# Own-chunk attention scores packed into half-width columns, in a scheduled four-layer kernel

## The chip, the cores and the metric

The program runs on one NeuronCore of a Trainium2 chip. A core has five engines with instruction queues of their own: TensorE (PE in the profile, with its weight loads apart as PEld), VectorE (DVE), ScalarE (ACT), GpSimd (POOL) and SyncE (SP, which here only issues DMAs). Each engine takes its instructions in order; between engines there are semaphores. The metric is the device time of one execution, in microseconds (us); lower is better.

## The reference

The input is x of 4 sequences, 512 positions, 128 channels. Four layers follow each other, each added to its input after a layer norm:

1. a power attention with 16 heads of 8 channels and a decay by gates;
2. a mixture of 8 experts (128 to 352 to 128 channels, each token goes to 2 of them);
3. a gated linear recurrence (called hgrn in the kernel);
4. the mixture of experts again, with the same weights.

The change is in the first layer. What it computes, cut to what matters:

```python
qkvgr = jnp.einsum('btc,oc->bto', x, W)          # q, k, v and one gate per head
log_G = jnp.cumsum(log_sigmoid(gates), axis=1)   # per head, over positions
S = jnp.einsum('bhtd,bhsd->bhts', Q, K)
Z = 2 * jnp.log(jnp.abs(S) + 1e-7) + log_G[..., :, None] - log_G[..., None, :] + const
Z = jnp.where(tril(ones((T, T))), Z, -inf)       # a target t sees the sources s <= t
P = jnp.exp(Z - rowmax)
y = einsum('bhts,bhsd->bhtd', P, V) / P.sum(-1)
```

Since the exponential undoes the logarithm, P is (|S| + 1e-7) squared times exp(log_G[t] - log_G[s]), up to a factor of the row that the division takes out. The kernel computes it in this form.

## The kernel before

**The plan.** All work is written as operations (`op`, L61) with the engines that may run it, a cost on each, what it reads and writes, and a priority. `Plan.run` (L138) writes out the instructions in an order that it finds with clocks of its own: `choose` (L200) gives an operation to the engine that would end it first by these costs plus `BIAS` (L26; DVE carries 0.3 us), and takes among those that can start the one with the lowest priority value. `room`, `pick` and `take` keep the buffers: kinds k2, k4, dec and others are lists of SBUF tiles, b1 is one of eight PSUM banks, b2 a pair of banks. An operation that opens a buffer waits in the plan until one is free. When PE would be idle for long in the plan, `lull` writes filler matmuls (L195). So costs, biases, priorities and buffer counts only decide the order and the engines; what runs then is fixed.

**Gates (`gates`, L583).** For each of the 4 sequences: layer norm, transposes, q, k, v and gates, the cumulated logs in three bf16 terms. These go through DRAM (`gd`) into the tile `gs` (L655, eight loads on SP's queue), which holds them as rows of a matmul with 6 rows, so that the matmul yields log_G[t] - log_G[s]. v stands in a tile `v` with 9 columns a head, the ninth being 1, for the norm. For sources of earlier chunks `vo` holds v with its decays multiplied in (L663).

**Attention (`attend`, L677).** A sequence has 4 chunks of 128 positions. `attend(b, g)` treats 4 heads of a sequence, one in each group of 32 partitions (L683 masks k for that); there are 16 attends, each released by the end of the one two before (`done`, L681). Scores lie with sources on partitions and targets in columns, heads in two pairs. The steps of one attend:

- `decay(half)` (L687), twice: a bf16 matmul puts the causal mask of 4 x 128 columns into a PSUM pair (L692), eight matmuls of 6 rows add the decay differences of the own chunk (L696), ACT takes the exponent of 2 x 512 columns into a `dec` tile (L701). A half stands for two chunks and all four heads.
- `scores(rnd)` (L707), three rounds: matmuls (L717) of source chunk 0 against all 4 target chunks (512 columns a head); of chunk 1 against 1 to 3 and chunk 3 against 3 (512); of chunk 2 against 2 and 3 (256). For each pair of heads the magnitude is taken out of PSUM by ACT (L728) or DVE (L729), and ACT squares it in place (L733).
- `fade(rnd, pr)` (L738): own-chunk columns are multiplied by the decays, in pieces of 2 x 128 columns on DVE or POOL (L744 and L749; eight in one attend).
- `values(jobs)` (L757): matmuls with v of 18 columns (two heads side by side) sum the result, own chunks into one PSUM bank (L771), earlier chunks into another (L775); six groups in one attend. Every second attend transposes and normalizes (from L806 to L842).

Own chunks are computed as full 128 x 128 squares, of which the mask leaves the lower triangle.

**The rest.** `route` (L863) places tokens by expert and sends them by indirect DMA on POOL (L1002); `experts` (L1040) runs up to 20 blocks of 128 tokens in each of 4 passes (L1088 first matmuls, L1107 transposes, L1112 second matmuls, L1125 the indirect DMA that sends results back); `combine` and `hgrn` (L1160) follow. The first pass of experts begins while the last sequence is in attention.

## Time and profile before

| | |
|---|---|
| time, median of 6 runs | 494.14 us (492.18 to 498.25) |
| the profiled execution | 494.13 us, span 492.4 us |
| PE busy | 428.6 us, 87% of the span |
| ACT busy | 341.2 us, 69% |
| DVE busy | 295.7 us, 60% |
| POOL busy | 246.6 us, 50% |
| attention's last square (L733) starts | 220.8 us |

The span runs from the first to the last instruction; the time is a little longer than it. Busy shares are means over the whole span, in which attention (the first 222 us or so) and the expert layers have different limits. A group in the profile names the line, the engine, the operation, what is written and read (partitions x columns) and how often; behind it stand busy time and the mean of one instruction, then the idle time ahead of them and who ended it. "issue" is idle time in which the engine waited for nothing that the profile shows. Buffer numbers are left out: a tile of k2 or k4 is called k, a PSUM bank ps. Records of fp32 matmuls come in twos for one matmul of the code.

### The profile page before, as it was taken

Reading aid. Unit: us, or ns where it says so; the run is one execution under the profiler, and the core shown is the slowest. Engines: PE = TensorE matmul, PEld = TensorE weight load, DVE = VectorE, ACT = ScalarE, POOL = GpSimd, SP = SyncE. Lnnn points to the kernel's source line nnn. Section 1 sums busy time; section 2 is a strip of 40 time slices with the busy share of each in tenths; the row PEclk is TensorE's granted clock in tenths of the full one; section 3 lists DMA queues with packets and bytes.
Section 4 is the critical chain, followed back from the end, with each engine's and each line's share of the span. In section 5 each row is a group of like instructions: output and inputs, shape, how many; then the busy total and the mean of one; then the engine's idle time right before and its main releaser. Section 6 shows DMA issues by size and latency. Waiting matters only on the chain.

```text
span 492.4 us, 10857 instructions
## 1 busy us (share of the span) xinstructions
PE 428.6 (87%) x3776; PEld 294.0 (60%) x3803; DVE 295.7 (60%) x896; ACT 341.2 (69%) x610; POOL 246.6 (50%) x399
## 2 busy tenths in 40 slices
PE   8899888878879889889899999979899989699960
PEld 7554445534545446447788767658666757478750
DVE  7865676857777687856721577880187894051212
ACT  5778999989987999997755564854445675146530
POOL 6353252563336322833488543488743567835540
PEclk9979999999998999999999999998989999799995
DMA  3047200174004910100113410012430011361004
GB/s 102 5 111 181 70 1 1 44 209 61 2 12 121 207 21 3 49 2 13 38 57 107 123 34 5 13 54 73 112 113 7 16 34 49 102 173 49 28 19 133
DMA packets 47070, 31.48 MB, mean 64 GB/s; under 512 B 6144, under 2 KB 44958, under 8 KB 47008
## 3 DMA queue, kind: packets, MB, share of 16 engines
q1 hardware_dynamic: 39232, 20.69, 17.8%
q0 software_dynamic: 4608, 8.44, 5.2%
q10 hardware_dynamic: 3168, 1.57, 1.1%
q8 instruction: 33, 0.54, 0.5%
q14 instruction: 29, 0.24, 0.2%
HBM read 15.73 MB, written 16.00 MB: 64 GB/s over the span
## 4 chain that ended last, share of the span: by engine, by line
PE 21%; POOL 15%; DVE 13%; issue 13%; ACT 12%; DMA 3%; POOLq 0%; DVEq 0%; SPq 0%; ACTq 0%
POOL yg L1125 8%; PE ps L1088 7%; ACT k L733 5%; PE ps L1112 4%; POOL xg L1002 3%; PE ps L1107 3%; ACT k L728 3%; PE ps L1169 2%; DMA k<-yg 2%; PE ps L717 1%; ACT dec L701 1%; POOL dummy L853 1%; DVE k L729 1%; ACT k L359 1%; POOL st L1211 1%
## 5 line engine op out<-in xcount | busy, mean ns | idle before, releaser
L1125 POOL DMA_INDIRECT yg<-y,xb x80 | 80.6, 1007 | 66.2 <-ACT y L1118 56.5
L1088 PE MATMUL ps<-we,k 128*128 x320 | 110.2, 472 | 1.1 <-issue 0.5
L733 ACT ACTIVATE k<-k,aeps 128x1024 f32<-128x1024 f32 (+1 forms) x96 | 92.0, 1006 | 0.8 <-DVE k L729 0.2
L1103 DVE TENSOR_TENSOR k<-k,ps 128x352 f32<-128x352 f32 x80 | 40.3, 515 | 84.5 <-PE ps L1088 82.6
L1002 POOL DMA_INDIRECT xg<-xk,slt x64 | 65.7, 1026 | 42.2 <-DVE slt L996 11.6
L359 ACT COPY k<-ps 128x384 f32<-128x384 f32 (+1 forms) x122 | 60.4, 511 | 35.9 <-PE ps L1107 20.4
L1112 PEld LDWEIGHTS ps<-we,k 128*128 128x128 f32 (+1 forms) x480 | 63.5, 196 | 11.9 <-ACT k L359 2.2
L1088 PEld LDWEIGHTS ps<-we,k 128*128 128x128 f32 x320 | 56.4, 194 | 23.1 <-issue 3.3
L1112 PE MATMUL ps<-we,k 128*128 (+1 forms) x480 | 66.8, 282 | 0.9 <-ACT k L359 0.6
L717 PE MATMUL ps<-k,k 32*128 32x384 f32 (+3 forms) x512 | 59.6, 474 | 3.0 <-ACT dec L701 1.3
L728 ACT ACTIVATE k<-ps 128x1024 f32<-128x1024 f32 (+1 forms) x53 | 47.4, 913 | 9.9 <-PE ps L717 9.9
L1100 ACT ACTIVATE k<-ps 128x352 f32<-128x352 f32 x77 | 35.4, 462 | 20.6 <-PE ps L1088 18.6
L729 DVE TENSOR_SCALAR k<-ps 128x1024 int32<-128x1024 int32 (+1 forms) x43 | 42.0, 982 | 11.5 <-PE ps L717 10.7
L744 POOL TENSOR_TENSOR k<-k,dec 128x256 f32<-128x256 f32 x30 | 26.5, 896 | 43.6 <-ACT k L733 34.9
L775 PE MATMUL ps<-k,vo 128*18 128x128 f32 x768 | 40.7, 283 | 8.0 <-ACT k L733 6.5
L1118 ACT ACTIVATE y<-ps 128x128 f32<-128x128 f32 x78 | 21.4, 277 | 36.9 <-PE ps L1112 34.0
L1107 PE MATMUL ps<-ident,k 128*128 128x128 f32 (+1 forms) x240 | 38.6, 281 | 7.6 <-DVE k L1103 4.0
L717 PEld LDWEIGHTS ps<-k,k 32*128 32x128 f32 x512 | 28.8, 186 | 19.1 <-ACT dec L701 4.7
L1107 PEld LDWEIGHTS ps<-ident,k 128*128 128x128 f32 (+1 forms) x240 | 27.9, 140 | 15.7 <-DVE k L1103 6.1
L775 PEld LDWEIGHTS ps<-k,vo 128*18 128x18 f32 x768 | 21.3, 99 | 24.9 <-ACT k L733 18.0
L771 PE MATMUL ps<-k,v 128*18 128x128 f32 x512 | 29.9, 285 | 5.6 <-POOL k L749 3.2
L701 ACT ACTIVATE dec<-ps 128x1024 f32<-128x1024 f32 x32 | 32.2, 1018 | 3.5 <-PE ps L696 3.0
(193 smaller groups left out, 640.3 us busy)
## 6 DMA issues: line engine op xcount, KB each, us to landing
xb<-xg SPq DMA_DIRECT2D x20, 258.0 KB
xg<-zero SPq DMA_DIRECT2D x8, 451.5 KB
k<-yg SPq DMA_DIRECT2D x12, 256.0 KB
we<-in_L_ffn_w_dram SPq DMA_DIRECT2D x8, 352.0 KB
xg<-zero SPq DMA_DIRECT2D x4, 387.0 KB
yg<-y,xb POOLq DMA_INDIRECT x80, 2.2
x<-in_L_attn_a_x_dram SPq DMA_DIRECT2D x4, 256.0 KB
we<-in_L_ffn_w_dram SPq DMA_DIRECT2D x8, 128.0 KB
```

Of the source, the lines that this page charges most:

```text
L359: e.copy(dst, src)
L717: e.matmul(sps[hh // 2].t[:, hh % 2, c : c + tn * P], kT.t[r, s * P : (s + 1) * P], qT.t[r, t0 * P : (t0 + tn) * P], start=True, stop=True)
L728: e.activation(view(), sps[pr].t[:, :, 0:n], AF.Abs)
L729: if e is nc.scalar else e.tensor_scalar(view().bitcast(I32), sps[pr].t[:, :, 0:n].bitcast(I32), 0x7FFFFFFF, None, ALU.bitwise_and)
L733: op({"ACT": act(2 * n)}, lambda e, pa=pa: e.activation(pa.t, pa.t, AF.Square, bias=aeps.t), r=[pa, aeps], w=[(pa, "o"), (pa, "d")], pri=p ...
L775: e.matmul(oo.t[rows, (i - 1) * P : i * P], s, p, start=(ev == 0 and (i, j) == (1, 0)), stop=(ev == 1 and j == i - 1), skip_group_check=True)
L1002: d = e.indirect_dma_start(out=xgv.t, out_offset=bass.IndirectOffsetOnAxis(ap=slot.t[:, k * NB + n : k * NB + n + 1], axis=0), in_=xk[k].t ...
L1088: e.matmul(ph.t[:, w, 0:HID], xT.t[:, k * P : (k + 1) * P], wf[:, bass.ds(regs[j] + w * HID, HID)], start=True, stop=True)
L1103: op({"DVE": ve(HID, True) + 0.03}, lambda e, ph=ph, sl=sl, h=h: e.tensor_tensor(h.t[:, 0:HID], sl.t[:, 0:HID], ph.t[:, 1, 0:HID], ALU.mul ...
L1107: e.transpose(hp.t[0:fn, f0 : f0 + P], h.t[:, f0 : f0 + fn], ident.t) for f0, fn in FCH
L1112: e.matmul(hp.t[:, NF_ * P : NF_ * P + C], hT.t[0:fn, kk * P : (kk + 1) * P], wf[0:fn, bass.ds(regs[j] + 2 * HID + kk * C, C)], start=(kk ...
L1125: d = e.indirect_dma_start(out=ygv.t, out_offset=bass.IndirectOffsetOnAxis(ap=xb.t[:, k, C : C + 1].bitcast(I32), axis=0), in_=y.t, in_off ...
```

## The change

Of an own chunk's square, the first 64 targets can see only the first 64 sources. The change computes, for each chunk, the last 64 targets against all 128 sources, and the first 64 targets against the first 64 sources; the latter fill only 64 partitions, so that those of an even and an odd chunk lie in the same columns, one on partitions 0 to 63, one on 64 to 127. Four own chunks take 4 x 64 + 2 x 64 = 384 columns a head in place of 512. With it change:

- the rounds: two of 512 columns; the columns of (3, 2) stand beside the own chunks, (2, 1) beside chunk 0's; (3, 1) goes into the 128 columns that are now spare in each decay pair, with a small tile (kind k1) of its own, whose magnitude only ACT takes;
- the decays: a half now stands for two heads with all own chunks; mask, exponent and `dec` tiles have 384 columns a head; `gs` is loaded by head and not by chunk;
- the fades: one per pair of heads, 2 x 384 columns;
- a tile `vs`: v of the first 64 positions of each chunk, for odd chunks on partitions 64 to 127 (four copies per sequence, and its memsets at the start); own-chunk values are 32 matmuls of 64 columns in one group, `near`;
- the plan: DVE's bias of 0.3 goes; operations of attention carry a term `lean` on one engine: 0.6 on ACT for magnitudes, 0.3 on ACT where else ACT is a choice, 0.3 on DVE where DVE and POOL are; several buffers of one kind are now looked for together; costs of PE, ACT and DVE are changed; exponents, spare magnitudes and squares get other priorities; k2 tiles are 12 and not 16, dec tiles 4 and not 3 (smaller).

The diff, without some cost constants, and from `ROUND` on without the removed lines (they stand in the kernel before):

```diff
-BIAS = {"PE": 0.0, "DVE": 0.3, "ACT": 0.0, "POOL": 0.0, "SP": 0.0}
+BIAS = {"PE": 0.0, "DVE": 0.0, "ACT": 0.0, "POOL": 0.0, "SP": 0.0}
...
+        self.lean = {}
...
-                n2 = [v for v in need if v.kind == "b2"]
-                if ok and len(n2) > 1 and len(self.room(n2[0])) < len(n2):
+                alike = [[v for v in need if v.kind == c] for c in {v.kind for v in need}]
+                alike = [vs for vs in alike if len(vs) > 1]
+                if ok and any(len(self.room(vs[0])) < len(vs) for vs in alike):
                     ok = False
                 if not ok:
                     if keep and at <= now + 2.0:
                         kept |= groups
                     continue
-                if len(n2) > 1:
-                    at = max(at, sorted(a for a, _, _, _ in self.room(n2[0]))[len(n2) - 1])
+                for vs in alike:
+                    at = max(at, sorted(a for a, _, _, _ in self.room(vs[0]))[len(vs) - 1])
                 for v in need:
                     at = max(at, self.pick(v, at)[0])
-            e = min(o.engs, key=lambda e: max(clock[e], at) + o.engs[e] + BIAS[e])
+            e = min(o.engs, key=lambda e: max(clock[e], at) + o.engs[e] + BIAS[e] + o.lean.get(e, 0.0))
...
+    vst = many("vs", 2, [P, NB, NH // 2, 3, HV])
+    HP, W3 = P // 2, 3 * P
...
-            "k2": many("k2_", 16, [P, T]),
+            "k2": many("k2_", 12, [P, T]),
+            "k1": many("k1_", 5, [P, 2 * P]),
             "k4": many("k4_", 6, [P, 2 * T]),
-            "dec": many("dec", 3, [P, 2 * T]),
-            "v": vt, "vo": ot, "gs": gst, "pad": padt,
+            "dec": many("dec", 4, [P, 2 * W3]),
+            "v": vt, "vs": vst, "vo": ot, "gs": gst, "pad": padt,
...
     def ve(n, ps=False):
-        return 0.12 + n * (0.00098 if ps else 0.0009)
+        return 0.14 + n * (0.00104 if ps else 0.0009)
 
     def act(n):
-        return 0.215 + n * 0.00071
+        return 0.16 + n * 0.00084
 
...
-    op({"DVE": ve(T)}, lambda e: e.tensor_copy(
-        negm4.t, negm.t.unsqueeze(1).to_broadcast([P, 4, P])), r=[negm], w=[negm4], pri=INIT)
+    op({"DVE": 0.35}, lambda e: e.tensor_copy(
+        negd.t[:, 0 : 2 * P].rearrange("p (n c) -> p n c", c=HP),
+        negm.t[:, HP:P].unsqueeze(1).to_broadcast([P, 4, HP])), r=[negm], w=[(negd, 2)], pri=INIT)
+    for h in range(2):
+        op({"DVE": 0.22}, lambda e, rows=slice(h * HP, (h + 1) * HP): e.tensor_copy(
+            negd.t[rows, 2 * P : W3].rearrange("p (n c) -> p n c", c=HP),
+            negm.t[rows, rows].unsqueeze(1).to_broadcast([HP, 2, HP])), r=[negm], w=[(negd, h)], pri=INIT)
...
+        for k, t in enumerate(vst):
+            op({"POOL": 0.9}, lambda e, t=t: (
+                e.memset(t, 0.0), e.memset(t[0:HP, 0::2, :, 0::2, HS:HV], 1.0),
+                e.memset(t[HP:P, 1::2, :, 0::2, HS:HV], 1.0)),
+               w=[slots_v[14 + k]], pri=INIT + 20 * k, after=mark)
...
+        for n in range(NB):
+            at = slice(n % 2 * HP, n % 2 * HP + HP)
+            op({"DVE": 0.27} if n % 2 else either(P), lambda e, n=n, at=at: copy(
+                e, vs.t[at, n, :, 0::2, 0:HS],
+                p4()[0:HP, n, 0:P].rearrange("p (m e d) -> p m e d", e=2, d=HS)),
+               r=[pr] + slots_v[14:16], w=[(vs, n)], pri=pri)
...
-        gv = lambda t: t.rearrange("p (g j n) -> p g j n", g=NG, n=NB)
-        ge = lambda: pg.t[:, 0:n0].rearrange("p (n j g) -> p g j n", n=NB, g=NG)
+        gv = lambda t: t.rearrange("p (j g n) -> p j g n", g=NG, n=NB)
+        ge = lambda: pg.t[:, 0:n0].rearrange("p (n j g) -> p j g n", n=NB, g=NG)
...
-            rows = lambda n=n: gd.t.rearrange("(h n) r t -> n r h t", n=NB)[n]
+            rows = lambda n=n: gd.t.rearrange("(j h) r t -> j r h t", j=4)[n]
             for u in range(2):
                 r0 = 32 * n + 3 * u
                 mark = sp(lambda e, r0=r0, u=u, rows=rows: e.dma_start(
-                    out=gs.t[r0 : r0 + 3, u].rearrange("p g (j t) -> p (g j) t", t=P), in_=rows()),
+                    out=gs.t[r0 : r0 + 3, u].rearrange("p g (n t) -> p (g n) t", t=P), in_=rows()),
...
+
+
+    NEAR = [(n * P, P, n * P + HP, 0, n * HP) for n in range(NB)]
+    NEAR += [(n * P, HP, n * P, n % 2 * HP, 2 * P + n // 2 * HP) for n in range(NB)]
+    ROUND = (
+        [(s0, sn, t0, HP, p0, c) for s0, sn, t0, p0, c in NEAR] + [(2 * P, P, W3, P, 0, W3)],
+        [(0, P, P, W3, 0, 0), (P, P, 2 * P, P, 0, W3)],
+    )
+    AT = {(1, 0): (1, 0), (2, 0): (1, P), (3, 0): (1, 2 * P), (2, 1): (1, W3), (3, 2): (0, W3), (3, 1): (2, 0)}
...
+        tiles = {}
+
+        def square(rnd, pa, n):
+            op({"ACT": act(n) + 0.13}, lambda e: e.activation(pa.t, pa.t, AF.Square, bias=aeps.t),
+               r=[pa, aeps], w=[(pa, "o"), (pa, "d")], pri=pri - 0.55 + 0.2 * rnd)
+
         def decay(half):
+
             pd = new("b2")
 
             def go(e):
                 for k in range(2):
...
+                    e.matmul(pd.t[:, k, 0:W3], identb.t, negd.t, start=True, stop=False)
+                for s0, sn, t0, p0, c in NEAR:
                     for k in range(2):
...
+                        r = 32 * (2 * half + k)
+                        e.matmul(pd.t[p0 : p0 + sn, k, c : c + HP], gs.t[r : r + 6, 0, g, s0 : s0 + sn],
+                                 gs.t[r : r + 6, 1, g, t0 : t0 + HP], start=False, stop=(c == 2 * P + HP))
+                for k in range(2):
+                    r = slice(32 * (2 * half + k), 32 * (2 * half + k) + 32)
+                    e.matmul(pd.t[:, k, W3:T], kT.t[r, P : 2 * P], qT.t[r, W3:T], start=True, stop=True)
+
+            pa = new("k1")
+            tiles[2, half] = (pa, lambda: pa.t.rearrange("p (u c) -> p u c", u=2))
+            op({"PE": 1.2}, go,
+               r=[identb, negd, kT, qT] + [(gs, (2 * half + k, u)) for k in range(2) for u in range(2)],
+               w=[pd], pri=pri - 0.4, after=start, hold=[dec[half], pa])
+            exps.append(op({"ACT": act(2 * W3)}, lambda e: e.activation(
+                dec[half].t.rearrange("p (k c) -> p k c", k=2), pd.t[:, :, 0:W3], AF.Exp),
+               r=[pd], w=[dec[half]], pri=pri - 1.4, table=("ln", "exp")))
+            op({"ACT": act(2 * P)}, lambda e: e.activation(tiles[2, half][1](), pd.t[:, :, W3:T], AF.Abs),
+               r=[pd], w=[pa], pri=pri - 1.4)
+            square(2, pa, 2 * P)
 
         def scores(rnd, pri):
...
+            n = T
             sps = [new("b2") for _ in range(2)]
...
+            pas = [new("k4") for _ in range(2)]
 
             def go(e):
...
+                for s0, sn, t0, tn, p0, c in ROUND[rnd]:
                     for hh in range(4):
                         r = slice(32 * hh, 32 * hh + 32)
...
+                        e.matmul(sps[hh // 2].t[p0 : p0 + sn, hh % 2, c : c + tn],
+                                 kT.t[r, s0 : s0 + sn], qT.t[r, t0 : t0 + tn], start=True, stop=True)
+
+            op({"PE": 0.95}, go, r=[kT, qT], w=sps, pri=pri, after=start, hold=pas)
             for pr in range(2):
                 pa = pas[pr]
                 view = lambda pa=pa: pa.t.rearrange("p (u c) -> p u c", u=2)
                 tiles[rnd, pr] = (pa, view)
...
+                mags.append(op(either(2 * n), lambda e, pr=pr, view=view: (
                     e.activation(view(), sps[pr].t[:, :, 0:n], AF.Abs)
                     if e is nc.scalar else e.tensor_scalar(
                         view().bitcast(I32), sps[pr].t[:, :, 0:n].bitcast(I32), 0x7FFFFFFF, None,
                         ALU.bitwise_and)
...
+                ), r=[sps[pr]], w=[pa], pri=pri + 0.05))
+                square(rnd, pa, 2 * n)
             return n
 
...
+        def fade(pr, pri):
+            pa, view = tiles[0, pr]
+            op({"DVE": ve(2 * W3) + 0.1, "POOL": 2.4}, lambda e: e.tensor_tensor(
+                view()[:, :, 0:W3], view()[:, :, 0:W3], dec[pr].t.rearrange("p (u c) -> p u c", u=2), ALU.mult),
+               r=[dec[pr], (pa, "d")], w=[(pa, "d")], pri=pri)
 
         if ev == 0:
             accs[b, m] = (new("b1"), new("b1"))
         od, oo = accs[b, m]
 
+        def lanes(t, k, hh):
+            return t[:, k, 2 * hh + m].rearrange("p k w -> p (k w)")[:, HV * ev : HV * ev + 2 * HV]
+
+        def near(pri):
+
+            jobs = [(vs, n, 2 * P + n // 2 * HP, 2 * n) for n in range(NB)] + [(v, n, n * HP, 2 * n + 1) for n in range(NB)]
+
+            def go(e):
+                for x, n, c, to in jobs:
+                    for hh in range(4):
+                        e.matmul(od.t[32 * hh : 32 * hh + 2 * HV, to * HP : (to + 1) * HP],
+                                 lanes(x.t, n, hh), tiles[0, hh // 2][1]()[:, hh % 2, c : c + HP],
+                                 start=(ev == 0 and to == 0), stop=(ev == 1), skip_group_check=True)
+
+            return op({"PE": 1.0}, go, r=[(tiles[0, pr][0], "d") for pr in range(2)] + [v, vs], w=[od], pri=pri)
+
         def values(jobs, pri):
...
             def go(e):
                 for i, j in jobs:
                     rnd, c = AT[i, j]
                     for hh in range(4):
...
+                        e.matmul(oo.t[32 * hh : 32 * hh + 2 * HV, (i - 1) * P : i * P],
+                                 lanes(o.t, pairs.index((i, j)), hh),
+                                 tiles[rnd, hh // 2][1]()[:, hh % 2, c : c + P],
+                                 start=(ev == 0 and (i, j) == (1, 0)),
+                                 stop=(ev == 1 and j == i - 1), skip_group_check=True)
+
+            return op({"PE": 0.26 * len(jobs)}, go, r=[(tiles[AT[j][0], pr][0], "o") for j in jobs for pr in range(2)] + [o],
+                      w=[oo], pri=pri)
 
         decay(0)
...
+        scores(0, pri - 1.0)
         decay(1)
...
+        scores(1, pri - 0.8)
         for pr in range(2):
...
+            fade(pr, pri)
+        values([(1, 0), (2, 0), (3, 0), (2, 1)], pri)
+        near(pri + 0.1)
+        done[n_] = values([(3, 1), (3, 2)], pri + 0.2)
...
+        for o in plan.ops:
+            if -5.0 < o.pri < 16.0 and len(o.engs) > 1:
+                o.lean = {"ACT": 0.6 if o in mags else 0.3} if "ACT" in o.engs else {"DVE": 0.3}
```

## The prediction

> **What bounds the kernel now.** First the slices of the page, to find the stages; each digit is the busy tenth of an engine in 12.3 us.
>
> ```profile
> PE   8899888878879889889899999979899989699960
> DVE  7865676857777687856721577880187894051212
> ACT  5778999989987999997755564854445675146530
> ```
>
> ACT stands at 8 and 9 from slice 5 to 18 and falls to about 5 behind it; PE is high everywhere. The costliest groups place that: scores, magnitudes, squares and decays (L701, L717, L728, L729, L733) all run in the first 222 us, the experts' matmuls (L1088, L1112) behind. So I read the engines' busy time in two long stretches (length, then PE, PEld, DVE, ACT, POOL):
>
> ```profile
> 30.00:222.00 192.00, 165.04 (x2204) 93.54 (x2229) 139.38 (x385) 176.22 (x235) 84.30 (x110) 0.97 0.31 70
> 222.00:477.00 255.00, 237.26 (x1367) 181.09 (x1367) 130.50 (x447) 144.44 (x337) 148.00 (x249) 0.97 0.20 59
> ```
>
> In attention ACT is busy 176.2 of 192 us (92%), PE 86%, DVE 73%. Behind it PE is, 237 of 255. Who waits decides whether 92% is a bound: the list of waits in 30 to 222 us.
>
> ```profile
> PEld ps L775 <- ACT k L733: 18.0, 32, 1.0
> DVE k L749 <- ACT k L733: 14.4, 24, 1.6
> PEld L696 <- issue: 14.0, 31, 0.8
> ...
> DVE k L729 <- PE ps L717: 10.2, 8, 3.6
> ACT k L728 <- PE ps L717: 9.2, 9, 2.8
> DVE k L744 <- ACT k L733: 9.1, 9, 2.0
> ```
>
> PE and DVE wait for ACT's squares again and again; ACT waits 9.2 us for scores and 3.0 for decays in the whole stage. Attention is ACT's stage, with PE a close second. The change acts here; what it takes from ACT counts, until PE or DVE comes last.
>
> **ACT's part.** The whole run's ACT groups, shapes kept apart (busy us, mean ns):
>
> ```profile
> L733 ACT ACTIVATE k<-k,aeps 128x1024 f32<-128x1024 f32 x64 | 70.7, 1150 | 0.5
> L728 ACT ACTIVATE k<-ps 128x1024 f32<-128x1024 f32 x40 | 40.0, 1019 | 8.7 <-PE ps L717 8.7
> ...
> L701 ACT ACTIVATE dec<-ps 128x1024 f32<-128x1024 f32 x32 | 32.2, 1018 | 3.5 <-PE ps L696 3.0 <-POOL dummy L853 0.5
> ...
> L733 ACT ACTIVATE k<-k,aeps 128x512 f32<-128x512 f32 x32 | 21.7, 717 | 0.4 <-DVE k L729 0.2
> ...
> L728 ACT ACTIVATE k<-ps 128x512 f32<-128x512 f32 x13 | 7.4, 587 | 1.2 <-PE ps L717 1.2
> ```
>
> I use busy over count, since followers overlap a little: out of PSUM 1.000 us for 1024 columns and 0.569 for 512, so 0.84 ns a column; squares 1.105 and 0.678, 0.83 ns a column. Per attend (16 of them) a pair of heads had 1280 columns a head in three rounds; it gets 1152.
> - Exponents of 768 in place of 1024: 1.006 - 0.216 = 0.79; 32 x 0.216 = **-6.9**.
> - Round 2's squares shrink from 512 to 256: 0.678 - 0.213 = 0.465; 32 x 0.213 = **-6.8**. The 64 large squares stay.
> - Round 2's magnitudes of 512 go: 13 on ACT, **-7.4**, 19 on DVE at 0.683, -13.0 there. In their place 32 magnitudes of 256, on ACT alone, out of the decays' spare columns: 0.569 - 0.215 = 0.354 each, **+11.3**.
>
> Sum on ACT -9.8 us with the 40 large magnitudes left where they are. This is the lower bound of ACT's relief.
>
> **DVE and POOL.** The fades were 83 of 256 columns on DVE (37.9 us, 0.457 each) and 45 on POOL. They become 32 of 768; by L1153 (0.685 for 512) a column costs 0.89 ns, so 0.91 each, 29.2 if all run on DVE. The new half copies of v are 16 at about the 0.274 of ACT's v copies: +4.3. DVE's sum: -13.0 - 37.9 + 29.2 + 4.3 = -17.4. That room is just what the planner's new terms may fill: DVE loses its bias of 0.3, ACT carries 0.6 against magnitudes and 0.3 against other choices. A large magnitude moved costs DVE 1.22 and saves ACT 1.00. Fourteen moves use up 17 us and take 14 more from ACT: -24 altogether. ACT's relief lies between 9.8 and 24; nothing in the trace says how many the order moves. I take the middle, 17, since DVE also has in-order waits and the fades are now all long.
>
> **PE's part.** From the timeline of 60 to 100 us (start, us, engine, line, tile shape, records; an fp32 matmul shows as two records):
>
> ```profile
> 61.89 0.22 PEld L696 LDWEIGHTS <-gst 6*128 6x128 bf16 x8 [0.42 <-issue]
> ...
> 65.12 1.14 PE L717 MATMUL ps<-k,k 32*128 32x512 f32 x8
> ...
> 66.19 0.41 PE L771 MATMUL ps<-k,v 128*18 128x128 f32 x8
> ...
> 71.76 0.85 PE L775 MATMUL ps<-k,vo 128*18 128x128 f32 x24 [0.21 <-ACT k L728]
> ...
> 80.18 1.06 PE L873 MATMUL ps<-gT,k 128*128 128x8 f32 x8
> ```
>
> - Scores. Three rounds took 1.14 + 1.15 + 0.70 = 2.99 us undisturbed. L873 moves 8 columns, so its records are nearly all weight load: (1.06 - 0.25) / 7 = 0.115 each. Round 0 now has, in each of four row groups, 8 loads with 64 columns to move (8 x 0.115 = 0.92), 8 of half the width (0.46), and the pair (3, 2) (0.21): 1.8 with a tail of 0.2. Round 1 stays 1.15; two spare-column pieces cost 0.4 each. Sum 3.75: +0.75.
> - Decays. The mask matmuls lose a quarter (-0.1 a half), the 16 small ones move as many columns as 8 did; a change of tile shape in the middle costs 0.21 (the shortest such idle) to 0.42. I take +0.4 per attend.
> - Near values. 8 records of 128 columns take 0.41, 24 take 0.85, so 0.22 for 8. 64 records of 64 columns then cost 0.88 like the 32 before, or 1.76 if a record is no cheaper for being short: 0 to +0.88; I take 0.2, as L771's eight run four abreast without a visible gap.
> - Fewer groups to switch between: two rounds for three, three value groups for six. Four switches gone at 0.21 pay for round 0's two.
>
> Sum +1.35 per attend, about 20 us over the 15 in this stretch. Against it stand 6.0 us of L195's filler matmuls, which are dropped when PE has work, and 10 us in which L717 counts 55.0 busy where 15 x 2.99 = 45 would do: its halves wait for a second PSUM pair, and an attend now takes six pairs in place of eight. PE: 165 + 20 - 16 = 169.
>
> [...]
>
> **What else moves.** One near step waits for both fades of tile 0, where four did for their own; behind it in PE's queue stand the last value group and the next attend's scores. L771's weights now wait 9.6 us for POOL in all; a fade of 768 on POOL costs at least 1.03 (L525, 512 columns) and by the planner 2.4, so a late one could idle PE a microsecond; the next attend is released two back, which covers most. I take 0, bound 16 x 0.5 = 8. The eight loads of gs per sequence on SP's queue keep number and bytes and only permute rows: 0. The two memset vs tiles go to POOL, 13.2 busy of the first 30 us: 0, at most 1. The negd copies replace one wide copy on DVE: 0. Gate 0's four half copies hold a PSUM pair up to 1.1 longer, before ACT is the bound: 0, at most 1. k2 falls from 16 tiles to 12; the order that the kernel before writes never holds more than 11 at once: 0. Exponents get an earlier priority; ACT is in order, so this exchanges, and adds nothing.
>
> Behind 222 us no work is changed, but the planner's biases and shorter PE costs reorder it. DVE (130 of 255) can take copies from ACT (144), neither is the bound; PE's 237 stay. 0, from -4 to +4.
>
> **Sum.** ACT 176 - 17 = 159, plus its 16 us of waiting, plus 5 more because PE at 169 now stands as near as ACT did: 180 for 192. So 492.4 - 12 = 480.4, with the 1.7 that lies around the span (494.13 - 492.4): **482**. The profiled execution equals the median of 494.14.
>
> **Rivals.**
> 1. Full balance: ACT -24, PE lets it: ACT 152 + 16 = 168, time 470. For: PE's waits are mostly for ACT. Against: PE's 169.
> 2. The gain is lost: large magnitudes stay with ACT (-9.8) and a half of that goes on near steps that wait for late fades, or the reordered experts lose up to 4. About 491, between 489 and 499. For: POOL and PE chains carry the second stage, its order is luck.
> 3. Slower: PE takes over. Its base without fillers and waits is 149. It decides when 149 + 15e passes 182 (192 less some 10 of unavoidable waits), at e = 2.2 us per attend. With short records no cheaper (+0.88), six shape changes at 0.21 (+1.26) and the 1.15 of scores and decays e is 3.3: 149 + 50 + 10 = 209 in place of 192 is the far end (511); half of the excess gives 503. For: PE already 86%, and every score record gets its own weight load. Against: 64-column records run beside each other in four groups.
>
> Chances: forecast 0.50 (474 to 489), full balance 0.17, gain lost 0.17, PE takes over 0.16. Faster by over 1% (what a measurement can tell from no change) 0.67, within 0.17, slower 0.16. The range leaves out half of the full balance (0.08) and the far part of rival 3 (0.11): 470 to 500.
>
> **What would show it.** ACT's exponents near 0.79 us with 768 columns, 32 magnitudes of 256 near 0.36, 64 large ones with over 33 on DVE, fades near 0.9; attention ending near 210; PE over 92% there. Wrong if scores in round 0 take over 2.5 us, if ACT waits for L717 or the decays more than 25 us, or if the stretch behind attention is not 255 us long.

## The result, and the profile after

The changed kernel takes 511.3 us (median of 20 runs, 503.3 to 522.6); the kernel before took 493.8 beside it. The ratio is 1.027 [1.025, 1.030] (in brackets the 95% interval): slower, where 482 us and faster were forecast. Ratios with an interval compare, within one set of runs, only those of each kernel within 1.5% of its fastest (the medians above alone would give 1.036), since the runs of one kernel spread and since in three of the five sets below every kernel, the one before too, took some 45 us longer (the one before 540 in place of 494). The profiled execution of the changed kernel took 503.8 us with a span of 502.0.

First the same slices as before, here with the clock that TensorE was granted (PEclk, tenths of full speed; "clock" below is this granted share); a slice is 12.5 us.

```profile
PE   8799998999897989899699999998999989599960
ACT  5388887797755785875455454673355774045430
PEclk9789998999876798889999999998999999899995
```

ACT has fallen to between 5 and 8 in nearly all of the first 18 slices, PE stands mostly at 9, and PEclk is 8 or less in ten of them, 6 or 7 in four. The two long stretches give it in numbers (length, PE, PEld, DVE, ACT, POOL, then the mean clock):

```profile
30.00:222.00 192.00, 179.19 (x3923) 135.16 (x3922) 148.91 (x358) 144.73 (x223) 71.43 (x77) 0.89 0.32 71
222.00:477.00 255.00, 238.48 (x1512) 185.38 (x1511) 142.97 (x471) 132.54 (x300) 144.87 (x243) 0.98 0.20 58
```

ACT is busy 31 us less in this stretch (176.2 to 144.7). Of these, 23 us are in the squares, exponents and magnitudes (161.8 to 138.8 us), near the far end of the forecast (24); the rest is copies and normed rows that the plan now gives to DVE. PE is busy 179 of 192, and its clock there fell from 0.97 to 0.89. ACT's and DVE's groups, shapes apart (busy us, mean ns, then idle before them), show that each step became as short as meant:

```profile
L716 ACT ACTIVATE k<-k,aeps 128x1024 f32<-128x1024 f32 x64 | 71.7, 1147 | 9.3 <-DVE k L766 8.9
...
L766 DVE TENSOR_SCALAR k<-ps 128x1024 int32<-128x1024 int32 x43 | 51.5, 1216 | 23.3 <-PE ps L756 23.0
...
L740 ACT ACTIVATE dec<-ps 128x768 f32<-128x768 f32 x32 | 25.8, 805 | 14.7 <-PE ps L733 14.3 <-issue 0.2
...
L743 ACT ACTIVATE k<-ps 128x256 f32<-128x256 f32 x32 | 12.1, 379 | 0.0
```

But the idle columns have turned round. Before, PE and DVE waited for ACT's squares; now the magnitudes wait for scores. In the list of waits from 30 to 222 us (engine, line, whom it waited for, us, times, longest):

```profile
DVE k L766 <- PE ps L756: 22.2, 14, 3.5
...
ACT dec L740 <- PE ps L733: 14.3, 14, 5.2
ACT k L765 <- PE ps L756: 11.4, 10, 2.7
```

The start of the eight additions of y to x (two in each sequence; L842 before, L861 after), read from the timeline, says where time was won and lost:

| us from the span's start | 1 | 2 | 3 | 4 | 5 | 6 | 7 | 8 |
|---|---|---|---|---|---|---|---|---|
| before | 49.3 | 70.6 | 104.2 | 123.8 | 159.9 | 178.0 | 208.0 | 227.6 |
| after | 55.1 | 74.0 | 104.0 | 121.8 | 166.7 | 180.0 | 208.4 | 228.2 |

Attention wins in some steps (the third takes 30.0 for 33.6, the sixth 13.3 for 18.1) and loses as much in others: 5.8 us by the first and 8.8 between the fourth and the fifth. In both PE stood still (3.19 us in front of L647, 3.43 us in front of L725) and then ran at half clock (10.2 and 13.7 us). The second of them in windows of 3.4 us (length, PE, PEld, DVE, ACT, POOL, clock):

```profile
151.40:154.80 3.40, 0.81 (x20) 0.62 (x21) 3.22 (x12) 2.23 (x5) 3.04 (x5) 0.99 0.06 19
154.80:158.20 3.40, 2.56 (x30) 1.71 (x33) 1.74 (x7) 0.35 (x1) 2.83 (x6) 0.50 0.20 62
158.20:161.60 3.40, 3.40 (x26) 2.88 (x22) 1.85 (x4) 2.27 (x5) 2.83 (x7) 0.50 0.13 40
161.60:165.00 3.40, 3.40 (x75) 2.92 (x75) 0.90 (x5) 3.23 (x6) 0.71 (x1) 0.50 0.12 39
165.00:168.40 3.40, 3.40 (x41) 2.71 (x42) 3.14 (x9) 3.40 (x4) 0.54 (x1) 0.50 0.32 90
168.40:171.80 3.40, 3.40 (x118) 2.59 (x106) 3.30 (x4) 0.74 (x2) 1.70 (x1) 1.00 0.29 73
```

PE is busy 0.81 of 3.40 us, and then stays at half clock for 13.7 us though it is busy in nearly all of them. Before, a pause at the same place (PE 1.07 of 3.40) cost one window:

```profile
144.00:147.40 3.40, 1.07 (x15) 1.01 (x19) 2.51 (x9) 2.77 (x4) 2.97 (x6) 0.99 0.13 42
147.40:150.80 3.40, 3.40 (x35) 1.17 (x24) 2.10 (x10) 1.38 (x3) 2.88 (x5) 0.50 0.19 60
150.80:154.20 3.40, 3.13 (x52) 1.91 (x45) 2.96 (x9) 3.40 (x5) 3.02 (x5) 1.00 0.52 152
```

What PE waited for in that pause is, by the profile, the copy L847, which comes late on DVE: ahead of it, behind the placing of tokens, stand four copies of v (13 of all 16 were ACT's before) and the four half copies that this change adds, 0.88 and 1.18 us (start, us, engine, line, operation):

```profile
153.19 0.88 DVE L366 COPY v<-ps 128x128 f32<-128x128 f32 x4
153.98 1.18 DVE L366 COPY vs<-ps 64x128 f32<-64x128 f32 x4
...
155.34 0.23 DVE L847 COPY yb<-ps 128x72 f32<-128x72 f32 x1
```

and PE's own line behind it:

```profile
155.64 0.80 PE L725 MATMUL ps<-negd,identb 128*128 128x384 bf16 x2 [3.43 <-DVE yb L847]
```

Counted from the clock's records in the trace, half clock between 30 and 222 us lasted 10.2 us before (6.8 and 3.4) and 41 after (6.8, 10.2, 13.7, 3.4 and 6.8). Behind the eighth addition no time is won back: 82 records of the experts' matmuls (L1088 and L1112 before) had started by 240 us before, 51 after, and the last result of the experts goes out at 486.9 in place of 477.3. That is the 9.6 us by which the span is longer.

So the spells of this trace last 3.4, 6.8, 10.2 and 13.7 us, and a window with PE busy throughout did not end them: the spell from 154.7 had three (3.40 of 3.40 us each).

### The profile page after: what moved, and what is told of

It reads as the page before. It is cut to its first block, busy times and chain, and to the rows that moved or that the text cites. A ratio compares the mean times of both kernels' runs of the same rounds, so it can differ in the third digit from the quotient of the medians.

```text
span 502.0 us, 14650 instructions
## 1 busy us (share of the span) xinstructions
PE 450.9 (90%) x5745; PEld 348.1 (69%) x5745; DVE 319.0 (64%) x894; ACT 296.7 (59%) x561; POOL 236.0 (47%) x372
## 5 line engine op out<-in xcount | busy, mean ns | idle before, releaser
L364 ACT COPY k<-ps 128x384 f32<-128x384 f32 (+1 forms) x95 | 47.6, 512 | 47.7 <-PE ps L1085 18.0
L766 DVE TENSOR_SCALAR k<-ps 128x1024 int32<-128x1024 int32 x43 | 51.5, 1216 | 23.3 <-PE ps L756 23.0
L756 PE MATMUL ps<-k,k 32*128 32x64 f32 (+3 forms) x1408 | 60.8, 320 | 1.0 <-issue 0.9
L756 PEld LDWEIGHTS ps<-k,k 32*128 32x128 f32 (+1 forms) x1408 | 47.2, 193 | 11.6 <-issue 3.8
L775 POOL TENSOR_TENSOR k<-k,dec 128x768 f32<-128x768 f32 x11 | 21.3, 1937 | 70.5 <-ACT dec L740 47.4
L366 DVE COPY k<-ps 128x384 f32<-128x384 f32 (+1 forms) x41 | 25.1, 612 | 27.5 <-PE ps L1126 21.6
L196 PE MATMUL ps<-ones 128*128 128x128 f32 x266 | 38.6, 293 | 0.0
L1126 PEld LDWEIGHTS ps<-ident,k 128*128 128x128 f32 (+1 forms) x240 | 27.6, 138 | 13.0 <-DVE k L1122 7.0
L196 PEld LDWEIGHTS ps<-ones 128*128 128x128 f32 x266 | 34.5, 203 | 2.3 <-issue 0.6
L740 ACT ACTIVATE dec<-ps 128x768 f32<-128x768 f32 x32 | 25.8, 805 | 14.7 <-PE ps L733 14.3
L765 ACT ACTIVATE k<-ps 128x1024 f32<-128x1024 f32 x21 | 21.2, 1022 | 14.1 <-PE ps L756 14.1
```

The source lines that it names most:

```text
L196: self.nc.tensor.matmul(self.pairs[i][2][:, h, 0 : self.idle.shape[1]], self.idle, self.idle, start=True, stop=True)
L364: e.copy(dst, src)
L756: e.matmul(sps[hh // 2].t[p0 : p0 + sn, hh % 2, c : c + tn], kT.t[r, s0 : s0 + sn], qT.t[r, t0 : t0 + tn], start=True, stop=True)
L766: if e is nc.scalar else e.tensor_scalar(view().bitcast(I32), sps[pr].t[:, :, 0:n].bitcast(I32), 0x7FFFFFFF, None, ALU.bitwise_and)
L1126: e.transpose(hp.t[0:fn, f0 : f0 + P], h.t[:, f0 : f0 + fn], ident.t) for f0, fn in FCH
```

## The experiments

For the first set of runs three theories stood. **A**: the loss is the clock, which drops after short pauses. **B**: PE is simply full, and fillers stand in its way. **C**: the planner's new preferences (no charge for DVE, 0.3 or 0.6 on ACT) pile work on DVE, so that PE pauses. The second set added **D**: the plan counts PE as free too early, since its costs for PE are too low. After it **E** took the place of B: PE's many short records cost more than their columns.

**First set (before: 539.7 us).** *No fillers*, the changed kernel:

```diff
-        if t1 - t0 < self.LULL or n < 1 or t0 < 2.5 or not free:
+        if True or t1 - t0 < self.LULL or n < 1 or t0 < 2.5 or not free:
```

> The kernel after without the planner's filler matmuls. Theory A (half-clock spells): in the profile of after the granted clock is 0.89 in 30 to 222 us where it was 0.97, which loses about 20 us of PE time; the fillers are what keeps it up elsewhere, so without them the clock falls further and the time rises to 515 or more. Theory B (the packed matmuls and the 34 us of fillers simply fill PE, the clock is an effect of that): without fillers PE gets up to 17 us back in attention and the time falls to about 495.

*Old preferences*, the changed kernel:

```diff
-BIAS = {"PE": 0.0, "DVE": 0.0, "ACT": 0.0, "POOL": 0.0, "SP": 0.0}
+BIAS = {"PE": 0.0, "DVE": 0.3, "ACT": 0.0, "POOL": 0.0, "SP": 0.0}
...
-        for o in plan.ops:
-            if -5.0 < o.pri < 16.0 and len(o.engs) > 1:
-                o.lean = {"ACT": 0.6 if o in mags else 0.3} if "ACT" in o.engs else {"DVE": 0.3}
```

> The kernel after with DVE's bias of 0.3 back and no lean: the packing with the planner's old preferences. Theory C (the new preferences pile copies, magnitudes and fades on DVE, PE stalls behind it at the gates and then runs at half clock): fewer stalls, clock back to 0.95 or more, time 485 to 494. Theories A and B say that the packing itself does it: time 500 or more, clock 0.93 or less.

*Warm decays*, the changed kernel:

```diff
             def go(e):
+                for _ in range(3):
+                    e.matmul(pd.t[:, 0, 0:P], ones.t, ones.t, start=True, stop=True)
                 for k in range(2):
                     e.matmul(pd.t[:, k, 0:W3], identb.t, negd.t, start=True, stop=False)
...
-            op({"PE": 1.2}, go,
+            op({"PE": 1.5}, go,
```

> The kernel after with three filler matmuls of 128x128 in front of each decay half (32 halves, 96 matmuls of 0.21 us, 20 us of PE time; they write columns that the mask overwrites). Theory A: clock in attention rises from 0.89 to 0.97 and wins about as much as the fillers cost or more: 495 to 504. Theory B: PE is full, so the time rises by the whole 20 us, to 520 or more.

*Planner alone*: the kernel before with the changed kernel's preferences and costs, nothing packed (the search for several buffers, the buffer counts and the other priorities stay as before; costs of transposes and experts' matmuls, which change too, are not shown):

```diff
-BIAS = {"PE": 0.0, "DVE": 0.3, "ACT": 0.0, "POOL": 0.0, "SP": 0.0}
+BIAS = {"PE": 0.0, "DVE": 0.0, "ACT": 0.0, "POOL": 0.0, "SP": 0.0}
...
-        return 0.12 + n * (0.00098 if ps else 0.0009)
+        return 0.14 + n * (0.00104 if ps else 0.0009)
...
-        return 0.215 + n * 0.00071
+        return 0.16 + n * 0.00084
...
+                o.lean = {"ACT": 0.6 if o in mags else 0.3} if "ACT" in o.engs else {"DVE": 0.3}
```

> The kernel before with the planner's part alone: bias 0, lean, the changed costs of DVE, ACT, transposes and expert matmuls; no packing. Theory C: slower than before by 5 us or more, with granted clock below 0.95. Theories A and B: within 1% of before (489 to 499).

Measured, as ratios to the kernel before: no fillers 1.038 [1.033, 1.044], clock 0.854 to 0.860; old preferences 1.045 [1.040, 1.050], clock 0.874 to 0.887; warm decays 578.9 us (569.7 to 581.9), that is 1.073 without an interval, clock 0.884 to 0.902; planner alone 1.018 [1.011, 1.025], clock 0.878 to 0.889 against 0.924 to 0.934 of the kernel before. So the preferences by themselves cost 1.8% and 0.04 of clock, which is C's claim; but taking them out of the changed kernel does not help (1.045), so C is not the whole. Fillers in front of the decays did not help. The changed kernel itself was not in this set, so how much the fillers are worth stayed open.

**Second set (before: 540.9 us).** The changed kernel unchanged, and three edits of it.

> The changed kernel unchanged, so that the three kernels beside it can be compared with it on one chip. Expected 1.02 to 1.035 of the kernel before, with a granted clock 0.03 to 0.05 below that of the kernel before.

*More fillers*:

```diff
-    LULL, PART, FILL = 0.6, 0.7, 0.22
+    LULL, PART, FILL = 0.35, 0.95, 0.2
```

> The changed kernel with fillers from planned lulls of 0.35 us on (0.6 before), filling 95% of the lull (70%). Theory A (the loss is the clock that drops after short pauses of PE): the clock between 30 and 222 us rises from 0.89 to 0.93 or more, and the time falls 5 to 12 us below the changed kernel of the same call. Theory B (PE is full, and fillers stand in the way of work): the fillers between 30 and 222 us grow from 16.7 to some 25 us, the clock stays below 0.91, and the time rises by 5 us or more.

*True PE costs*:

```diff
-            op({"PE": 0.95}, go, r=[kT, qT], w=sps, pri=pri, after=start, hold=pas)
+            op({"PE": 1.95 if rnd == 0 else 1.3}, go, r=[kT, qT], w=sps, pri=pri, after=start, hold=pas)
...
-            return op({"PE": 1.0}, go, r=[(tiles[0, pr][0], "d") for pr in range(2)] + [v, vs], w=[od], pri=pri)
+            return op({"PE": 1.15}, go, r=[(tiles[0, pr][0], "d") for pr in range(2)] + [v, vs], w=[od], pri=pri)
...
-            op({"PE": 1.2}, go,
+            op({"PE": 1.3}, go,
```

> The changed kernel with the planner's costs for PE near what the trace shows: scores of round 0 1.95 us (0.95 before), of round 1 1.3 (0.95), decays 1.3 (1.2), near values 1.15 (1.0). Theory D (the planner takes PE to be free 1.5 us per attend too early, and so orders ACT and DVE for a schedule that does not happen): fewer fillers, and 5 us or more faster than the changed kernel of the same call. Theory A (clock alone): the fillers between 30 and 222 us fall below 12 us, the clock does not rise, and the time stays within 1% or gets longer.

*Lean for magnitudes only*:

```diff
-BIAS = {"PE": 0.0, "DVE": 0.0, "ACT": 0.0, "POOL": 0.0, "SP": 0.0}
+BIAS = {"PE": 0.0, "DVE": 0.3, "ACT": 0.0, "POOL": 0.0, "SP": 0.0}
...
-                o.lean = {"ACT": 0.6 if o in mags else 0.3} if "ACT" in o.engs else {"DVE": 0.3}
+                o.lean = {"ACT": 0.6 if o in mags else 0.0} if "ACT" in o.engs else {}
```

> The changed kernel with the preference for DVE kept for the 64 large magnitudes alone; all other operations weigh DVE and ACT as in the kernel before (DVE charged 0.3 us more). Theory C (the block's normed rows, v and vs copies pile up on DVE where a block starts or ends, PE waits 2 to 3.5 us for gates, queries or y, and the clock halves for 6 to 14 us after each): DVE is busy 8 to 15 us less between 30 and 222 us, the waits of PE for DVE fall by 3 us or more, the clock there rises to 0.92 or more, and the time falls by 5 to 10 us. Rival: the pauses are spread over all steps of a crowded schedule and only move: the clock stays within 0.02, and the time within 1%.

Measured: unchanged 1.047 [1.042, 1.051], clock 0.865 to 0.875; more fillers 1.067 [1.063, 1.070], clock 0.882 to 0.894; true costs 1.032 [1.028, 1.036], clock 0.864 and 0.867; lean for magnitudes only 1.015 [1.009, 1.020], clock 0.883 to 0.888. Here a higher clock went with a longer time once (more fillers, for which A had expected 5 to 12 us less) and with a shorter one once (lean), so the clock alone does not order them. With more fillers PE had 25.1 us of them between 30 and 222 (16.3 unchanged, 9.7 with true costs), and the three times go in that order, as B and D had said. The lean helped most: DVE was busy 301 us in place of 317. It goes to C that part of the loss comes from work that the preferences need not have moved.

The profiles of this set show a thing that the first ones hardly have: pauses in which PE waits for no one. PE's lines of the unchanged kernel from 108 us on:

```profile
108.56 0.82 PE L725 MATMUL ps<-negd,identb 128*128 128x384 bf16 x2
109.31 0.28 PE L729 MATMUL ps<-gst 6*128 6x64 bf16 x3
109.96 0.30 PE L729 MATMUL ps<-gst 6*128 6x64 bf16 x4 [0.37 <-issue]
111.38 0.40 PE L729 MATMUL ps<-gst 6*128 6x64 bf16 x4 [1.12 <-issue]
112.80 0.29 PE L729 MATMUL ps<-gst 6*64 6x64 bf16 x4 [1.02 <-issue]
```

Sixteen small matmuls that take 0.47 us otherwise come in fours, half a microsecond to one apart. Pauses of PE over 0.25 us in front of an instruction that waits on no semaphore, counted in the trace: one in the kernel before (0.5 us) and four in the changed kernel (4.0 us) in the executions profiled first, 22 here (17.3 us), 15 of them while POOL's indirect DMAs follow each other within 3 us (these stretches cover 229 of 572 us). Planner alone, with the long records and in the first set, had one (0.5 us). So by these counts they take both, small records and a set in which every kernel takes some 45 us longer.

**Third set (before: 494.2 us).** Now each side of the change alone. *Small records alone*, the kernel before:

```diff
-                        e.matmul(pd.t[:, k, t], gs.t[r : r + 6, 0, g, t], gs.t[r : r + 6, 1, g, t],
-                                 start=False, stop=(hh == 3))
+                        for c in (hh * P, hh * P + 64):
+                            e.matmul(pd.t[:, k, c : c + 64], gs.t[r : r + 6, 0, g, t],
+                                     gs.t[r : r + 6, 1, g, c : c + 64], start=False, stop=(c == 3 * P + 64))
...
+                        for a, b_ in ((0, 64), (64, P), (P, tn * P)):
+                            if a < b_:
+                                e.matmul(sps[hh // 2].t[:, hh % 2, c + a : c + b_],
+                                         kT.t[r, s * P : (s + 1) * P], qT.t[r, t0 * P + a : t0 * P + b_],
+                                         start=True, stop=True)
...
+                            for a in (0, 64):
+                                e.matmul(od.t[rows, i * P + a : i * P + a + 64], s, p[:, a : a + 64],
+                                         start=(ev == 0 and i == 0 and a == 0), stop=(ev == 1),
+                                         skip_group_check=True)
```

> The kernel before with only PE's records cut as small as the change makes them, nothing packed and nothing moved: every score matmul in pieces of 64, 64 and the rest, every decay and every near-value matmul in two of 64 columns (88, 32 and 64 records per attend for 32, 16 and 32, so that about 230 instead of 132 pairs of weight load and matmul come per attend). ACT, DVE and POOL have the work of before, and the planner's costs and order stay. Theory E (the change loses on PE's side: many short records, which take longer than their columns and whose instructions come late) says 1.02 or more of the kernel before, with PE 10 us or more busier between 30 and 222 us and pauses of PE that wait for nothing. Theory C (the loss comes from the planner's preferences, which pile work on DVE) says within 1%.

*Relief alone*, the kernel before with ACT's and the fades' work of the change; it leaves out a quarter of the decays, half of the last round and two of eight fades, so it does not compute the function:

```diff
-            exps.append(op({"ACT": act(2 * T)}, lambda e: e.activation(
-                dec[half].t, pd.t.rearrange("p k t -> p (k t)"), AF.Exp),
+            exps.append(op({"ACT": act(6 * P)}, lambda e: e.activation(
+                dec[half].t.rearrange("p (k t) -> p k t", k=2)[:, :, 0 : 3 * P], pd.t[:, :, 0 : 3 * P], AF.Exp),
...
+            n = min(n, T) if rnd < 2 else P
...
-                for k in range(2):
+                for k in range(1):
                     op(flex(2 * P), lambda e, k=k: e.tensor_tensor(
```

> The kernel before with only the work of ACT and of the fades cut to what the change leaves: exps of 768 instead of 1024 columns, magnitudes and squares of round 2 of 256 instead of 512, six of the eight fades of 256 columns per attend. It leaves out a quarter of the decays, half of the last round and two fades, and takes wrong data for them. PE's records, the planner's preferences and its order of costs are those of before. Theory E (ACT bounds the kernel before, and the change would have gained had PE's side cost nothing) says 0.965 to 0.985 of the kernel before. The rival (ACT was no bound, PE or the clock sets the pace already) says within 1%.

*Lean and costs*: the second set's last two edits together. *The same without fillers*: with the first set's line in `lull` as well.

> The changed kernel with both edits that helped alone: the preference for DVE for the large magnitudes only (1.0146 alone) and the truer costs of PE (1.0318 alone, the changed kernel 1.0465 on that chip). If the gains add up: 1.00 or below. If both remove the same pauses: 1.01 to 1.02.

> The run beside it without any filler of PE. Theory A (fillers keep the clock up): slower than the run beside it by 1% or more, with the clock 0.03 or more lower. Theory E (a filler is one more pair of instructions for PE to be fed with): faster by 0.5 to 1.5%, with a clock no more than 0.03 lower.

Small records alone: 530.4 us (515.6 to 549.7), 1.04 to 1.11 of the kernel before, with ACT's and DVE's work untouched. Its page's PE line and its stretch of attention:

```profile
PE 472.3 (91%) x5437; PEld 365.8 (70%) x5467; DVE 295.2 (57%) x896; ACT 344.1 (66%) x610; POOL 244.8 (47%) x399
```

```profile
30.00:222.00 192.00, 181.85 (x3398) 141.58 (x3423) 128.78 (x366) 163.16 (x218) 77.43 (x103) 0.94 0.30 70
```

PE 472 in place of 429: this kernel overstates the change (451), since it cuts the scores in 64 columns throughout; its score group is busy 108.2 us, against 59.6 before and 77 after (60.8 of L756 and 16.3 of L733). Its four runs spread by 34 us, and the longer times have the lower clock: 515.6 at 0.940, 522.5 at 0.939, 538.3 at 0.897, 549.7 at 0.877. E had also expected pauses that wait for nothing; there are four (2.3 us), no more than in the changed kernel.

Relief alone: 0.990 [0.987, 0.993]. In it ACT's exponents take 0.80 us, and ACT is 17 us less busy in attention:

```profile
30.00:222.00 192.00, 170.39 (x2157) 96.20 (x2181) 124.43 (x360) 159.11 (x229) 73.73 (x105) 0.90 0.30 70
```

```profile
DVE k L730 <- PE ps L717: 17.9, 14, 3.2
...
ACT k L729 <- PE ps L717: 15.1, 13, 3.6
```

ACT fell to 159.1, as the forecast had it for the change (159), with PE's records as they were but for fewer fillers (14 for 38 records in this stretch); and the kernel won 4 us, not 12. Waits for PE's scores grew: 10.2 to 17.9 us on DVE, 9.2 to 15.1 on ACT. This is the run that speaks most clearly on the forecast's first step.

It also shows that the relief lowers the clock by itself: 0.90 in attention in place of 0.97, with half clock for 37.5 us in place of 10.2, and 0.947 in place of 0.965 over the whole run (medians). One of its spells, in windows of 3.4 us as above, is as long as the longest of the changed kernel, with no record cut:

```profile
134.40:137.80 3.40, 2.32 (x47) 1.66 (x49) 3.12 (x13) 1.95 (x5) 1.41 (x2) 1.00 0.00 0
137.80:141.20 3.40, 3.04 (x33) 1.55 (x32) 2.99 (x17) 3.37 (x7) 0.35 (x1) 0.50 0.03 7
141.20:144.60 3.40, 1.38 (x12) 0.69 (x9) 1.89 (x8) 2.70 (x5) 3.02 (x6) 0.50 0.12 39
144.60:148.00 3.40, 3.40 (x45) 2.54 (x48) 2.17 (x10) 0.98 (x2) 2.83 (x6) 0.50 0.18 58
148.00:151.40 3.40, 3.40 (x23) 1.17 (x27) 1.43 (x4) 1.74 (x3) 2.73 (x5) 0.50 0.47 136
151.40:154.80 3.40, 3.13 (x42) 1.88 (x42) 2.46 (x8) 3.18 (x5) 0.19 (x1) 0.99 0.38 96
```

Lean and costs: 504.2 us (499.2 to 512.3), 1.020 of the kernel before; without fillers 515.4 (510.6 to 523.2), 1.043. These two hold the same records and differ in fillers alone. Their page lines for all engines, with fillers first, then without:

```profile
PE 444.2 (89%) x5697; PEld 341.4 (68%) x5697; DVE 300.9 (60%) x849; ACT 312.7 (63%) x614; POOL 228.0 (46%) x368
```

```profile
PE 438.6 (86%) x5479; PEld 326.0 (64%) x5479; DVE 301.0 (59%) x849; ACT 313.6 (61%) x614; POOL 228.4 (45%) x368
```

The group of fillers is busy 31.0 us in the first, so PE's own records take 444.2 - 31.0 = 413.2 us there at a mean clock of 0.937, and 438.6 at 0.882. 413.2 x 0.937 / 0.882 = 439.0: the same work, longer by just the clock. So a lower clock has a price here: taking the fillers out lowers it by 0.055 and makes the kernel 11 us slower. That the change itself loses in this way is A's claim, and this pair does not show it. By the same sum PE's own records took 428.6 - 17.1 = 411.5 us before at 0.962, and 450.9 - 38.6 = 412.3 after at 0.926; at the clock of before the latter would be 397. In the sets in which the kernel before took 540 us, the same fillers did not help (1.038 without them, 1.047 with them, in two sets).

**Fourth set (before: 540.4 us).** How much of the loss is PE's side at its real price.

*Records at the change's cost*: as small records alone, but with `((0, P), (P, tn * P))` for the three pieces of a score matmul.

> The kernel before with PE's records cut, as in the run with small records alone, but the score matmuls only in pieces of 128 columns and the rest (56 records per attend for 32), so that PE's busy time grows about as much as in the changed kernel (its 451 us against 429); decays and near values in halves as there. ACT, DVE, POOL, planner and order as before. Theory E (PE's side alone loses what the change loses): 1.015 to 1.03 of the kernel before, with PE 15 to 25 us busier. If the loss of the run with small records alone (515 to 550 us) was only its dearer scores (104 us of PE against 56): within 1%.

*Small decays and near values*: the same with whole score matmuls.

> The run beside it with the scores whole again: only decays and near values in halves (32 and 64 records per attend for 16 and 32). By the prediction's terms (decays +0.4, near +0.2 us per attend, 10 us in all, of which PE had 27 us room) within 1%. Theory E with the many small records of decays as what drops the clock: 1.01 or more, and a granted clock 0.02 or more below that of the kernel before.

*Lean for magnitudes only* once more, and the unchanged changed kernel beside it:

> The changed kernel with the preference for DVE for the large magnitudes only, again, since it was the best version of the changed kernel (1.0146 against 1.0465 for the changed kernel beside it). 1.000 to 1.015 of the kernel before, and 1.5% or more faster than the changed kernel of this call. Below 0.995 it would beat both kernels.

> The changed kernel unchanged, for the comparison with the three beside it. 1.02 to 1.045 of the kernel before; its runs lie on one line of time against granted clock, some 5 us longer for each 0.01 of clock less.

Records at the change's cost 1.015 [1.008, 1.022], small decays and near values 1.013 [1.006, 1.020], both with clocks of 0.920 to 0.929, hardly below the kernel before (0.915 to 0.936); the cut score matmuls of the first add nothing that can be told. Lean 1.019 [1.011, 1.028], the unchanged one 572.2 us (562.5 to 575.3), 1.059 without an interval. So the halved decays and near values cost 1.3% with the clock hardly changed; by what way was not found. The lean is again better than the changed kernel (550.4 and 553.3 us in its faster runs, against 562.5 in the fastest of the other) and again slower than the kernel before.

**Fifth set (before: 494.2 us).** Whether the clock took the relief's gain: relief alone with more fillers and with none (the edits of the second and first set on it).

> The kernel before with the relief alone (its quarter of the decays, half of the last round and two fades left out, as in the run with relief alone), and with fillers from planned lulls of 0.35 us on, filling 95% of them. If the clock ate what the relief gave (0.942 to 0.958 there, 0.953 to 0.973 in the kernel before), it is back at 0.96 or more and the time is 0.975 to 0.985 of the kernel before. If the relief is worth no more than 1% because ACT was not what set the pace, the time stays at 0.985 to 0.995 whatever the clock.

> The run with relief alone without any filler. Clock as cause: the granted clock falls by 0.04 or more below the run beside it and the time is longer by 8 us or more. Clock as a mere sign of pauses: the clock falls and the time stays within 1% of the run beside it.

0.989 [0.983, 0.996] at clocks of 0.944 to 0.962, and 0.992 [0.989, 0.996] at 0.915 to 0.948. The relief is worth 1% with either. Attention, with more fillers first, then with none:

```profile
30.00:222.00 192.00, 176.25 (x2229) 99.47 (x2233) 126.09 (x363) 161.36 (x232) 75.27 (x107) 0.92 0.31 70
```

```profile
30.00:222.00 192.00, 172.21 (x2221) 94.89 (x2220) 126.54 (x364) 161.87 (x235) 76.30 (x108) 0.93 0.31 70
```

Neither brought the clock of attention back to 0.97: half clock there lasted 30.7 and 27.3 us, against 10.2 in the kernel before. So the question stays open. Within each kernel the time does go with the clock: the ten runs without fillers reach from 488.2 us at 0.946 to 495.8 at 0.915, about 2.1 us for each 0.01 by a straight line through them, and the fastest with more fillers is 486.6 at 0.962, the clock of the kernel before.

What else takes the gain can be read in part in the run without fillers: the seventh addition of y to x starts at 197.8 us in place of 208.0, the eighth at 226.5 in place of 227.6, and 30 records of the experts' matmuls have started by 222 us in place of 15. Ten microseconds are won up to the seventh addition and nine of them spent before the eighth, where PE has records of the experts in its queue and runs 3.4 us at half clock (before: none). By 240 us the lead in the experts' records is 86 to 82, and the end comes 4 us sooner. How much of the ten went to the experts and how much to the clock is not separated.

## Why the prediction was wrong

**The step that failed first** is the one from ACT's relief to time: "attention is ACT's stage, with PE a close second", and the sum that it led to, 192 to 180. ACT's part held term by term: exponents 0.805 us (0.79 forecast), 32 magnitudes of 256 at 0.379 (0.354), 64 large squares unchanged at 71.7, 43 large magnitudes on DVE (over 33), fades on DVE 0.97 (0.91). But 17 us off ACT alone won 4 us, where 12 were forecast. The waits in the profile, PE and DVE on ACT, were true; they were not what set the end. Why 8 us are missing stays open between two readings. In one, ACT at 92% and PE at 86% waited for each other in turn, and over the whole span PE, busy 87%, holds the work that has to be emptied: argued from where the relief's ten microseconds went. In the other the relief lost them to the clock, which it lowered: without fillers the median is 0.936 in place of 0.963, and at 2.1 us for each 0.01 that is an estimate of 5.7 us. It is an upper one, since a pause ahead of half clock takes time of its own (3.43 us ahead of the 13.7 in the changed kernel). The rival "the gain is lost" (489 to 499) had the time of the relief alone, 490.4, but not its reason.

**PE's part** came near in total by offset, not by its terms. Round 0 of the scores took 1.97 us at full clock (1.8 forecast, the limit set was 2.5), and 3.4 at half clock. Without fillers PE was busy 179.2 - 16.7 = 162.5 us between 30 and 222, below the forecast's 169. By groups over the whole run, the scores grew from 59.6 to 77.1 us, where the forecast's 16 x 3.75 makes 60; the decays took 32.4 (27.5 before, where 27 of the 64 mask matmuls have no record in the trace); the near values fell from 29.9 to 18.0, where a rise of 3 was forecast; and the values of earlier chunks, which had no term, fell from 40.7 to 27.6. Together that is 157.7 or more before and 155.1 after, where some 20 us more were forecast. That the total came near the forecast is luck.

The second step that failed is a term that was left out: the granted clock, which the windows had in their sixth column, 0.97 in attention before and 0.89 after. Two terms stood on it. Fillers were to be dropped when PE has work: they rose from 6.0 to 16.7 us there, as the plan holds PE for free when it is not (it charges 0.95 us for a round of scores that takes 1.97; with true costs they fell from 16.3 to 9.7). And the half copies of v, for which 0, at most 1, was put: at 152 us they stand in the pause of 3.43 us that begins 13.7 us of half clock.

**The planner's part** was costed at 0, from -4 to +4, and only behind 222 us. Alone, on the kernel before, it costs 1.8%, in a set in which that kernel took 540 us.

**The sum of the parts**, as ratios: relief 0.990, records 1.015, planner 1.018; their product is 1.023, against 1.027 [1.025, 1.030]. The second and third were measured in sets in which all kernels ran longer, so that the product comes so near is no proof, and they don't simply add: the changed kernel without the preferences is no faster (1.045), the one with them for magnitudes only is (1.015 and 1.019). So the parts are shown singly; how they share the loss in the changed kernel is not. The clock fell with the planner alone (0.885 for 0.929, medians) and with the relief (0.947 for 0.965), and by less than 0.01 with the records at the change's cost.

**How much is the clock.** The 22 recorded runs of the changed kernel go from 503.3 us at 0.931 to 522.6 at 0.893: 19.3 us for 0.038, or 5.1 us for each 0.01. Pauses ahead of half clock, like the one of 3.43 us, take time of their own, so this is an upper price. The pair with and without fillers gives 11 us for 0.055, 2.0 us for each 0.01. For the 0.036 between the two profiled runs that makes 7 to 18 us of the 22 by which the profiled run missed the forecast. The rest would be the relief that was worth 4 and not 12, as far as its own loss is not the clock as well.

**Rival 3** (PE takes over, 503, far end 511) is where the time ended, by another way. Its point of decision was 2.2 us more of PE per attend; PE's own records grew by 0.8 us in the whole run (411.5 to 412.3) and not by 3.3 an attend. Its 1.26 us an attend for shape changes, 20 us in 16 attends, hardly shows in PE's idle time: in front of the near values and the scores this was 2.2 and 1.0 us in the whole run.

**The rest.** Attention ended at 228.2 us, not near 210. ACT waited 25.7 us for L756 and L733, past the 25 that was set as a sign of error. The work behind attention ended 9.6 us later: of the experts' records the kernel before had begun 31 more at 240 us.

## What to carry to other kernels

Before an engine's relief is turned into time, ask which engine has to be emptied over the whole span, and test the relief alone: leave the work out and measure. Where TensorE is near full, read its granted clock beside its busy time: the same round of scores took 1.97 us at full clock and 3.4 at half, some pauses of 1 to 3 us were followed by 10 to 14 us of half clock, and a change that only relieved ACT lowered the clock too. Packing that saves columns on one engine but cuts another's matmuls into short records had a price in records here (108.2 us for scores cut throughout, where they took 59.6), and a hand-made order needs their true cost before it may choose.

## What had not been expected of the hardware

- Half clock lasted in steps of 3.4 us (spells of 3.4 to 23.9 us), and it did not end because PE was busy. In the kernel before a pause with PE busy for a share of 0.30 of 3.4 us was followed by one such step; in the changed kernel pauses with 0.48 and 0.26 were followed by 10.2 and 13.7 us with PE busy 0.99 and 0.93 of them. In the run with small records alone half clock began at 217.8 us, after two windows with PE busy 0.90 and no pause over 0.42 us, and lasted 23.9 us with PE busy 0.98. It came without short matmuls as well: with the long score, decay and value records of the kernel before, relief with more fillers had 10.2 us from 84.9 us on with PE busy throughout, and planner alone 17.1 us from 155.6 on with PE busy 0.95. What decides when a spell ends was not found.
- Runs of one kernel can spread along the granted clock: 3 us for the kernel before in the third set (493.5 to 496.3), 13 for lean and costs and 34 for small records alone beside it, 19 for the changed kernel, mostly longer with the lower clock. Short records alone did not make the spread: records at the change's cost and small decays and near values spread by 3.4 and 4.3 us, the kernel before beside them by 6.7.
- In sets in which the kernel before took 540 us, PE's instructions came late: in the changed kernel's run of the second set 22 pauses, 17.3 us in all, that waited for nothing the profile shows, 15 of them during POOL's indirect DMAs, with small matmuls issued four at a time. That PE was fed too slowly is argued; what set those sets apart from the others is open. Single instructions of ACT took the same time there (1.021 us for the large magnitude, 1.022 in the changed kernel's first profile).
